# One written order for all engines in a test-time-trained linear layer and the feed-forward work laid between its rounds

## The chip, the cores and the metric

The kernel runs on one core of a Trainium2 chip. The time is the device time of one execution in microseconds (us); of several runs the median is given. PE is the matrix engine (TensorE), PEld its weight loads, DVE the vector engine, ACT the scalar engine, POOL GpSimd, SP the engine that issues most of the transfers.

## The reference

The program is a chain of eight blocks on `x` of shape (2, 1024, 256), each added to `x` after a normalization: two attention layers with a feed-forward each, a differential attention with a feed-forward, and at the end a linear model that is trained while it runs ("test-time training", TTT) with a last feed-forward. The change touches the TTT layer and the feed-forwards around it. Cut to what matters, for chunks of 16 tokens and 16 heads of width 16:

```python
def step(S, inp):                      # one chunk; 64 of them, one after the other
    qi, ki, vi, ei = inp
    kh = einsum('bchd,bhde->bche', ki, S)
    target = vi - ki
    mu = mean(kh, -1)
    rstd = rsqrt(var(kh, -1) + EPS)
    kh_hat = (kh - mu) * rstd
    g = w * kh_hat + b - target
    gw = g * w
    v_new = (gw - mean(gw, -1) - kh_hat * mean(gw * kh_hat, -1)) * rstd
    A = where(tri, einsum('bchd,bshd->bhcs', qi, ki), 0.0) * ei
    qh = einsum('bchd,bhde->bche', qi, S) - einsum('bhcs,bshe->bche', A, v_new)
    o = qi + _ln(qh, w, b)
    S = S - einsum('bchd,bche->bhde', ki * ei, v_new)
    return S, o
# before: q = silu(x Wq), k = x Wk scaled to unit length per head, v = x Wv,
#         beta = 2 sigmoid(x Wbeta)
# after:  o * sigmoid(x Wg1 Wg2), an RMS norm per head, then @ Wo
# feed-forward: (gelu(x Wg) * (x Wu)) @ Wd, 2048 hidden columns
```

The state `S` makes the 64 chunks a serial chain.

## The kernel before

Five stages follow each other; the last, `ttt_ffn1` (L1520), is the one in question. It has eight tiles of 2 x 128 tokens. Each tile has eight **rounds**, one per chunk of all heads, so there are 64 rounds. The pieces of work are closures that are called in some order:

- `ttt_inputs` (L1668) makes a tile's inputs: `begin` (normalization: statistics and root on DVE, scaling on POOL), `turn` (transposes, then ACT to `xT`), `keys` (projection to q and k, unit length of k), `targets` (values, then 16 small transfers `uk_d<-uk` through DRAM and one back into `r`, from which POOL makes `kp`), `diagonals` (transposes of k and q to `kqT`), `weights` (the products of keys and queries inside a chunk, `pa`, copied to `ag`), `low_ranks`, `rates`.
- `ttt_step` (L1859) is the heart of a round. `kh` is made of two products on PE, one from the state and one from the step `vs` before; ACT squares it, and some twenty small DVE operations follow (`rsqrt` alone has nine) to the new step `vs`.
- Around it a round has three more products of 16 small matmuls each (32x32 weights, 16 columns): the output's part from the state, `ds` for the state's update, and the output's part from `vs`. `ttt_product` (L1657) writes each of these; a product shows as 32 matmul instructions, and all as L1663.
- `ttt_outputs` (L1902) takes a finished tile through DRAM (17 transfers), normalizes it twice around the gate (`normalize`, nearly all on DVE), transposes and projects it, and adds it to `x`.
- `ffn1_tile` (L1959) is the feed-forward of a tile: `rows`, `turn`, eight `hidden` pieces (gate and up matmuls on PE, gelu on ACT, product on DVE) and four `down` pieces of eight matmuls.

In round n the products stand in the order output-from-state, `kh` from state, `kh` from `vs`, `ds`, output-from-`vs`; then come the pieces of `fill[n]` (L1615), written out by hand: outputs of the tile before, inputs of the tile after, and feed-forward of the tiles behind. The feed-forward of the previous layer's last tile is `owed`: its first three hidden pieces are laid between the inputs of tile 0, the rest in the rounds of the first two tiles.

Only PE runs in the written order here (L1590). DVE, ACT and POOL are ordered by the scheduler of the language, which takes what is ready by its own model and lays instructions of independent pieces between each other. The stages before use `in_order()` (L335), which holds PE, DVE, ACT and POOL in the written order. The SP queue is never held by hand.

The buffer for normalized tokens, `xT`, has two copies, and the PSUM buffer `gen`, through which most input and output pieces pass, has two.

Of the kernel before, what the change touches and what calls it, by code (L numbers as in the profile page):

```python
# [10 lines left out]
F32 = mybir.dt.float32  # L11
# [3 lines left out]
ALU = mybir.AluOpType  # L15
# [24 lines left out]
def interleave_into(out, a, b):  # L40
# [58 lines left out]
    "unpack": (-7.9, 2.57, (6.7, 7.6, 10.3, 13.8)),  # L99
}  # L100


class Net:
# [1416 lines left out]
    def ttt_ffn1(self, w, deq):  # L1520
# [11 lines left out]
        with ExitStack() as ctx:  # L1532
# [57 lines left out]
            ctx.enter_context(tc.manual_schedule(engines={mybir.EngineType.PE}))  # L1590
            data, inputs = self.ttt_inputs(0)
            owed = self.ffn1_tile(NB - 1, deq)
            begin, turn, keys, targets, diagonals, ag01, ag23, low_ranks, rates = inputs
            for piece in (
                begin, turn, keys, owed[0], targets, owed[1], diagonals, owed[2], ag01, owed[3],
                ag23, low_ranks, owed[4], rates,
            ):
                piece()
            vs = self.ttt_step(0, data, None)
            outputs = ffn = last_ffn = [lambda: None] * 20  # L1600
            nothing = [lambda: None]
            owed_by_tile = [
                nothing * 5 + [
                    owed[5], *nothing, owed[6], *nothing, owed[7], *nothing, owed[8], *nothing,
                    owed[9],
                ],
                nothing * 8 + [*nothing, owed[10], *nothing, *owed[11:14]],
            ]
            for i in range(NB):
                next_data, inputs = None, [lambda: None] * 9  # L1610
                if i < 2:
                    last_ffn = owed_by_tile[i]
                if i + 1 < NB:
                    next_data, inputs = self.ttt_inputs(i + 1)
                fill = [  # L1615
                    [outputs[0], inputs[0], *last_ffn[5:7], inputs[1]],
                    [last_ffn[7], inputs[2]],
                    [*last_ffn[8:10], inputs[3]],
                    [last_ffn[10], inputs[7], outputs[1]],
                    [last_ffn[11], outputs[2], ffn[0], inputs[4]],  # L1620
                    [last_ffn[12], inputs[8], inputs[5], inputs[6]],
                    [last_ffn[13], ffn[1], ffn[2]],
                    [ffn[3], ffn[4]],
                ]
                pq = ps.tile([P, 8, 4, D], F32, tag="pq", name="pq")
                for n in range(8):
                    S, vs_n = t.S, vs
                    self.ttt_product(
                        pq[:, n], lambda g: data.kq[:, 2 * n + 1, g, :], lambda g: S[:, g, :],
                        n == 0,  # L1630
                    )
                    if n < 7:
                        vs = self.ttt_step(n + 1, data, vs_n)
                    ds_ = ps.tile([P, 4, D], F32, tag="ds", name="ds")
                    self.ttt_product(
                        ds_, lambda g: data.kp[:, 4 * n + g, :], lambda g: vs_n[:, g, :],
                        True, True,
                    )
                    t.S = work.tile([P, 4, D], F32, tag="S", name="S", bufs=3)
                    nc.vector.tensor_tensor(t.S, S, ds_, ALU.add)  # L1640
                    self.ttt_product(
                        pq[:, n], lambda g: data.ag[:, n, g, 0, :], lambda g: vs_n[:, g, :], False
                    )
                    if n == 7:
                        qh = work.tile([P, 8, 4, D], F32, tag="qh", name="qh")
                        nc.scalar.copy(qh, pq)
                        if i + 1 < NB:
                            vs = self.ttt_step(0, next_data, None)
                    for piece in fill[n]:
                        piece()  # L1650
                outputs = self.ttt_outputs(i, data, qh)
                last_ffn, ffn = ffn, self.ffn1_tile(i, deq)
                data = next_data
            for piece in outputs[:1] + last_ffn[5:14] + outputs[1:] + ffn:
                piece()
# [12 lines left out]
    def ttt_inputs(self, i):  # L1668
# [5 lines left out]
        t_ = type("tile", (), {})()  # L1674
# [3 lines left out]

        def begin():
            t_.xn = self.layernorm_rows(work, (i, NB + i))  # L1680

        def turn():
            pt = gen("ln_t").rearrange("p (k t) -> p k t", k=2)
            t_.xT = self.layernorm_turn(work, pt, t_.xn, False)

        def to_diagonal(kind, src, scale):

            pt = gen("kq_t").rearrange("p (g n c) -> p n g c", g=4, c=D)
            for b in range(B):
                by_f = work.tile([P, 2, 8, D], F32, tag="by_f", name="by_f")  # L1690
                nc.scalar.activation(
                    by_f.rearrange("p f h d -> p h f d"), src(b), AF.Copy, scale=scale
                )
                for f in range(2):
                    nc.tensor.transpose(
                        pt[:, :, 2 * b + f, :], by_f[:, f].rearrange("p h d -> p (h d)"),
                        self.ident,
                    )
            for j in range(2):
                nc.scalar.activation(  # L1700
                    t_.kqT[:, :, kind, :, j, :], pt, AF.Copy, scale=t.half[:, j : j + 1]
                )

        def keys():
            q = t_.q = work.tile([P, B, C], F32, tag="q", name="q")
            k = work.tile([P, B, C], F32, tag="k", name="k", bufs=1)
            uk = t_.uk = work.tile([P, B, 8, 2, 2, D], F32, tag="uk", name="uk", bufs=1)
            for b in range(B):
                pqk = gen("pqk")
                self.project(pqk, t_.xT, b, w["wqkv"], 0, 512)  # L1710

                nc.scalar.activation(q[:, b], pqk[:, 0:C], AF.Tanh, scale=0.5)
                nc.vector.scalar_tensor_tensor(
                    q[:, b], q[:, b], 1.0, pqk[:, 0:C], ALU.add, ALU.mult
                )
                nc.scalar.copy(k[:, b], pqk[:, C : 2 * C])
            sq = work.tile([P, B, C], F32, tag="sq", name="sq", bufs=1)
            rk = work.tile([P, 32], F32, tag="rk", name="rk")
            nc.scalar.activation(sq, k, AF.Square)
            nc.vector.tensor_reduce(  # L1720
                rk, sq.rearrange("p b (h d) -> p (b h) d", d=D), AX.X, ALU.add
            )
            rk = self.rsqrt(work, rk, 1.0, 1e-6, "rk")
            nc.vector.tensor_scalar_mul(rk, rk, -1.0)
            kn = uk[:, :, :, :, 1, :].rearrange("p b h f d -> p (b h f) d")
            nc.vector.tensor_tensor(
                kn, k.rearrange("p b (h d) -> p (b h) d", d=D),
# [3 lines left out]
        def targets():  # L1731
            uk = t_.uk

            un = uk[:, :, :, :, 0, :].rearrange("p b h f d -> p b (h f) d")
            nc.vector.tensor_tensor(
                un, uk[:, :, :, :, 1, :].rearrange("p b h f d -> p b (h f) d"),
                w["ln_w"].rearrange("p (h d) -> p h d", d=D).unsqueeze(1)
                .to_broadcast([P, B, 16, D]), ALU.mult,
            )
            pv = gen("pv")  # L1740
            for b in range(B):
                out = pv[:, b * C : (b + 1) * C]
                nc.tensor.matmul(out, t.ones, t.wb, start=True, stop=False)
                for kc in range(2):
# [3 lines left out]
                    )  # L1748
            nc.vector.tensor_tensor(
                un, un, pv.rearrange("p (b n d) -> p b n d", b=B, d=D), ALU.add  # L1750
# [13 lines left out]
            )  # L1764
            kp = work.tile([P, 32, 2, D], F32, tag="kp", name="kp")
            for j in range(2):
                nc.gpsimd.tensor_scalar(
                    kp[:, :, j, :], r[:, :, 1, :], t.half[:, j : j + 1], 1.0, ALU.mult, ALU.mult
                )
            t_.kp = kp.rearrange("p m j d -> p m (j d)")  # L1770

        def diagonals():
            t_.kqT = work.tile([P, 8, 2, 4, 2, D], F32, tag="kqT", name="kqT")
            t_.kq = t_.kqT.rearrange("p n k g j c -> p (n k) g (j c)")
            to_diagonal(0, lambda b: t_.uk[:, b, :, :, 1, :], 1.0)
            to_diagonal(
                1, lambda b: t_.q[:, b, :].rearrange("p (h f d) -> p h f d", f=2, d=D), 0.5
            )
# [4 lines left out]
            t_.ag = work.tile([P, 8, 4, 2, 32], F32, tag="ag", name="ag")  # L1783

        def weights(pairs):

            ag, kq = t_.ag, t_.kq
            for pair in pairs:
                pa = gen("pa").rearrange("p (n g k c) -> p n g k c", n=2, g=4, k=2)
# [169 lines left out]
    def ffn1_tile(self, i, deq):  # L1959
# [7 lines left out]
        def rows():  # L1967
            f.xn = self.layernorm_rows(work, (i, NB + i))
# [190 lines left out]
```

## Time and profile before

| | us |
|---|---|
| median of 3 runs | 2913.81 (2906.41 to 2915.19) |
| profiled execution | 2906.75 |
| its span | 2905.0 |
| PE busy in the span | 2530.3 (87%) |
| DVE busy in the span | 2003.4 (69%) |
| `qh` copied at the end of tile 0 | 2198.7 |
| `qh` copied at the end of tile 7 | 2806.5 |

The stage under change begins at about 2090 us, when the stage before has added its last projection to `x` (DVE L1403 at 2089.31). The copy of `qh` marks the end of each tile's rounds; all eight lie at 2198.7, 2284.0, 2372.5, 2466.1, 2554.1, 2643.0, 2738.6 and 2806.5. After the last one stands the remaining feed-forward.

In the views that follow, a row of the table by stretches gives for each engine its busy time and, in brackets, its number of instructions; behind the engines stand the granted PE clock as a share of full speed, the share of busy DMA engines and the GB/s they moved. In the table of waits a row gives the waiting engine and line, what it waited for, the sum in us, how often, and the longest. "issue" is a wait for nothing that the profile shows. In a timeline a row gives start, duration, engine, line and operation.

### The profile page before, as it was taken

Reading aid. Unit: us, or ns where it says so; the run is one execution under the profiler, and the core shown is the slowest. Engines: PE = TensorE matmul, PEld = TensorE weight load, DVE = VectorE, ACT = ScalarE, POOL = GpSimd, SP = SyncE. Lnnn points to the kernel's source line nnn. Section 1 sums busy time; section 2 is a strip of 40 time slices with the busy share of each in tenths; the row PEclk is TensorE's granted clock in tenths of the full one; section 3 lists DMA queues with packets and bytes.
Section 4 is the critical chain, followed back from the end, with each engine's and each line's share of the span. In section 5 each row is a group of like instructions: output and inputs, shape, how many; then the busy total and the mean of one; then the engine's idle time right before and its main releaser. Section 6 shows DMA issues by size and latency. Waiting matters only on the chain.

```text
span 2905.0 us, 66838 instructions
## 1 busy us (share of the span) xinstructions
PE 2530.3 (87%) x26384; PEld 1572.5 (54%) x26384; DVE 2003.4 (69%) x6786; ACT 1329.8 (46%) x2800; POOL 1021.7 (35%) x1568
## 2 busy tenths in 40 slices
PE   6999998999998877988888888888787988898888
PEld 2334334444434444665555555555565776777777
DVE  5777774866758957778777878787657555665551
ACT  2676870345453335666666666757321211221110
POOL 3444242211106757667555655655300000000000
PEclk9999998999999967999999999999887998999999
DMA  3000000000001100000000000000011010110100
GB/s 121 1 1 1 1 1 0 1 1 1 1 1 53 36 1 1 1 1 1 1 1 1 1 1 1 1 1 1 20 31 25 10 25 21 21 31 18 24 9 15
DMA packets 61978, 35.37 MB, mean 12 GB/s; under 512 B 43216, under 2 KB 58080, under 8 KB 61664
## 3 DMA queue, kind: packets, MB, share of 16 engines
q1 hardware_dynamic: 59472, 29.49, 3.9%
q8 instruction: 207, 3.39, 0.5%
q10 hardware_dynamic: 2192, 1.61, 0.2%
q14 instruction: 107, 0.88, 0.1%
HBM read 22.68 MB, written 8.39 MB: 11 GB/s over the span
## 4 chain that ended last, share of the span: by engine, by line
PE 39%; DVE 13%; ACT 4%; POOL 4%; issue 4%; DMA 0%; POOLq 0%; ACTq 0%; DVEq 0%
PE ph L1484 5%; PE po L1993 5%; PE pg L1980 5%; PE pu L1980 4%; DVE p L1247 4%; PE e L1236 4%; PE dT L1308 3%; PE po L1503 2%; DVE p L1286 2%; PE py L1338 1%; POOL p L1294 1%; ACT p L1257 1%; POOL p L1274 1%; PE pq L1663 1%; PE kh L1663 1%
## 5 line engine op out<-in xcount | busy, mean ns | idle before, releaser
L1257 ACT ACTIVATE p<-p,nm 128x128 f32<-128x128 f32 (+7 forms) x512 | 390.8, 767 | 78.7 <-DVE nm L1253 40.9
L1247 DVE CUSTOM_DVE_ANT_0 p<-e,mask 128x512 f32<-128x512 f32 (+3 forms) x768 | 382.1, 551 | 59.5 <-PE e L1236 59.1
L1294 POOL TENSOR_SCALAR p<-p,md 128x128 f32<-128x128 f32 (+7 forms) x256 | 241.0, 945 | 175.5 <-DVE md L1286 147.4
L254 POOL TENSOR_SCALAR ln_mv<-ln_mv 128x2 f32<-128x2 f32 x64 | 15.7, 246 | 722.5 <-DVE ln_mv L252 709.6
L1322 ACT ACTIVATE pT<-dT 128x384 f32<-128x384 f32 (+3 forms) x384 | 176.2, 486 | 202.1 <-PE dT L1308 201.2
L1236 PE MATMUL e<-kT,qT 32*128 32x512 f32 (+3 forms) x1536 | 229.8, 578 | 44.3 <-DVE nm L1247 41.5
L1308 PE MATMUL dT<-ident,p 128*128 128x128 f32 x1152 | 197.0, 297 | 65.8 <-POOL p L1294 35.6
L1286 DVE CUSTOM_DVE_ANT_0 p<-p,nrs 128x128 f32<-128x128 f32 (+7 forms) x256 | 220.3, 885 | 24.7 <-POOL p L1278 24.4
L901 ACT ACTIVATE pr<-s 128x512 f32<-128x512 f32 (+3 forms) x384 | 157.3, 497 | 162.9 <-PE s L896 154.2
L1274 POOL TENSOR_SCALAR p<-p,ra,neg_lam 128x128 f32<-128x128 f32 (+7 forms) x256 | 217.8, 851 | 9.3
L1308 PEld LDWEIGHTS dT<-ident,p 128*128 128x128 f32 x1152 | 137.6, 149 | 153.1 <-POOL p L1294 67.7
L617 ACT ACTIVATE pr<-s 128x1024 f32<-128x1024 f32 (+1 forms) x192 | 145.3, 813 | 131.0 <-PE s L611 83.5
L1993 PE MATMUL po<-down,inter 128*128 128x256 f32 x576 | 160.1, 441 | 1.9 <-DVE x L2000 1.2
L861 PE MATMUL s<-kT,qT 32*128 32x512 f32 (+3 forms) x768 | 155.3, 519 | 3.8 <-DVE q_pad L869 1.9
L1980 PE MATMUL pg<-xT,gate 128*128 128x256 f32 x576 | 151.1, 409 | 5.5 <-ACT xT L283 5.5
L622 ACT ACTIVATE pr<-pr 128x1024 f32<-128x1024 f32 (+1 forms) x192 | 152.1, 852 | 0.0
L869 DVE CUSTOM_DVE_ANT_0 masked<-s,mask 128x128 f32<-128x128 f32 (+3 forms) x256 | 110.6, 487 | 58.9 <-PE s L861 58.8
L1236 PEld LDWEIGHTS e<-kT,qT 32*128 32x128 f32 x1536 | 84.8, 202 | 116.4 <-DVE nm L1247 74.3
L625 POOL TENSOR_SCALAR_AFFINE_SELECT pr<-pr 128x256 f32<-128x256 f32 x128 | 90.1, 722 | 154.7 <-ACT pr L622 57.7
L1986 DVE TENSOR_TENSOR inter<-inter,pu 128x512 f32<-128x512 f32 x72 | 49.3, 684 | 132.7 <-PE pu L1980 132.7
L1993 PEld LDWEIGHTS po<-down,inter 128*128 128x128 f32 x576 | 126.4, 224 | 25.0 <-DVE x L2000 2.0
L1980 PE MATMUL pu<-xT,up 128*128 128x256 f32 x576 | 139.3, 386 | 0.0
(295 smaller groups left out, 5377.2 us busy)
## 6 DMA issues: line engine op xcount, KB each, us to landing
uk_d<-uk SPq DMA_DIRECT2D x128, 32.0 KB, 1.9
r<-uk_d SPq DMA_DIRECT2D x8, 512.0 KB, 3.6
x<-in_L_attn_a_X SPq DMA_DIRECT2D x4, 512.0 KB, 6.9
qh_d<-qh SPq DMA_DIRECT2D x8, 256.0 KB, 2.6
o<-qh_d SPq DMA_DIRECT2D x128, 16.0 KB, 1.7
out<-x SPq DMA_DIRECT2D x4, 512.0 KB, 3.1
w<-in_L_ffn_W2T SPq DMA_DIRECT2D x1, 1024.0 KB, 7.5
pk<-in_L_ffn_gate_packed SPq DMA_DIRECT2D x8, 128.0 KB, 2.5
```

The source lines that it names most:

```text
L861: nc.tensor.matmul(tiles[g][:, 0:n], shared["qT"][rows, t, j * P : (j + 1) * P], kT[rows, lo : lo + n], start=True, stop=True,)
L901: nc.scalar.activation(pr[:, g, off:512], tiles[g][:, 0:m], AF.Exp, scale=0.25)
L1236: nc.tensor.matmul(own.tiles[h][:, a, 0 : hi - lo], made["q"][r : r + 32, a, t, :], kT[r : r + 32, a, lo:hi], start=True, stop=True,)
L1247: nc.vector.tensor_tensor_reduce(own.p[h][a][:, lo:hi], own.tiles[h][:, a, 0 : hi - lo], neg_row[:, T - nk + lo : T - nk + hi], -1.0, 3e38 ...
L1257: nc.scalar.activation(own.p[h][a], own.p[h][a], AF.Exp, bias=own.nm[:, h, a : a + 1], scale=-1.0, accum_out=own.sm[:, h, a : a + 1],)
L1274: nc.gpsimd.tensor_scalar(p1, p1, own.ra[:, h : h + 1], nlam[:, head : head + 1], ALU.mult, ALU.mult)
L1286: nc.vector.tensor_tensor_reduce(p0, p0, p1, own.nrs[:, h : h + 1], 3e38, ALU.add, ALU.min, own.md[:, h : h + 1],)
L1294: nc.gpsimd.tensor_scalar(p0, p0, -1.0, own.md[:, h : h + 1], ALU.mult, ALU.add)
L1308: nc.tensor.transpose(dT[:, n, :], own.p[h][0][:, kb * P : (kb + 1) * P], self.ident)
L1322: nc.scalar.activation(shared[t, s + h][:, lo:hi, :], own.dT[h, part][:, 0 : hi - lo, :], AF.Exp)
L1980: nc.tensor.matmul(ph[:, j, :], m_[:, kc, m * P : (m + 1) * P], f.xT[:, kc, :], start=(kc == 0), stop=(kc == 1),)
L1993: nc.tensor.matmul(f.po[:, b], inter[m // 2][:, m % 2, b * P : (b + 1) * P], wd[:, m % 2, (m // 2) * C : (m // 2 + 1) * C], start=(m == 0) ...
```

## The change

All four engines are held in the written order for the whole stage. For this the pieces are split where they change engine, so that a DVE part can stand later than the PE part that it reads: 32 pieces of inputs, 12 of outputs, 28 of feed-forward. A table gives each piece a time in rounds, relative to its tile; the ten parts of a round have fixed places 0.0 to 0.9 in it, and pieces are sorted among them.

- The round is now `K` (`kh` from state), `Q` (output from state), `k` (`kh` from `vs`), `q` (output from `vs`), `d` (`ds`), then the DVE parts `0` (ACT square, sum), `1` (root), `s` (state), `2` (gradient), `3` (finish to `vs`).
- The four `pa` products, before in one round, stand at 5.718, 7.26, 7.93 and 9.56 of the tile's time.
- `un = kn * ln_w` of the targets and the two operations `o * w_out`, `o + q` of the output gate go from DVE to POOL.
- `down` has eight pieces of four matmuls instead of four of eight; `xT` has four copies; `by_f` has one buffer per half.
- The feed-forward that is owed gets its own row; only its normalization and transposes stand ahead of round 0.

The diff, cut:

```diff
+TTT = {
+    "round": "K Q k q d 0 1 s 2 3",
+    "inputs": (
+        0.71, 1.04, 1.918, 1.923, 2.086, 2.518, 2.955, 2.923, 3.183, 3.82, 4.025, 2.963,
+        4.43, 5.74, 4.325, 4.74, 3.21, 5.132, 5.34, 5.718, 5.955, 7.26, 7.54, 7.93, 8.455,
+        9.56, 10.065, 3.663, 4.623, 5.719, 5.983, 6.765,
+    ),
+    "outputs": (0.58, 0.585, 1.55, 1.555, 1.66, 2.086, 2.6, 2.7, 2.958, 3.69, 4.43, 4.786),
+    "ffn": (
+        5.02, 5.025, 5.66, 6.618, 6.969, 7.618, 7.623, 9.118, 9.123, 9.618, 9.623, 10.618,
+        10.869, 11.55, 11.769, 12.518, 13.169, 13.618, 13.623, 7.774, 8.71, 9.95, 10.67,
+        11.974, 11.979, 13.674, 13.979, 14.084,
+    ),
...
+    "owed": (
+        -28.5, -25.1, -22.6, 1.263, 2.1, 2.43, 3.927, 3.932, 4.69, 5.645, 6.2, 7.709,
+        7.714, 8.663, 9.955, 10.527, 11.6, 11.865, 12.869, 3.932, 4.54, 6.946, 7.747, 9.96,
+        11.32, 13.23, 13.87, 14.91,
+    ),
+}
...
-            ctx.enter_context(tc.manual_schedule(engines={mybir.EngineType.PE}))
+            ctx.enter_context(self.in_order())
...
+                for m, step in zip(times, inputs):
+                    add(n + m if i else m - 30, step)
+                n += 16
+                outputs = self.ttt_outputs(i, data)
...
+            for n in range(8 * NB):
+                i, m = n // 8, n % 8
+                steps = self.ttt_round(i, m, tiles)
+                tokens = TTT["round"].split()
+                fill = sorted(at.pop(n, []), key=lambda x: x[0])
+                for k, token in enumerate(tokens):
+                    while fill and (fill[0][0] - n) * len(tokens) <= k + 1e-6:
+                        fill.pop(0)[1]()
+                    if token in steps:
+                        steps[token]()
+                for _, step in fill:
+                    step()
...
+        def by_w():
+
             for b in range(B):
+                nc.gpsimd.tensor_tensor(
+                    t_.uk[:, b, :, :, 0, :].rearrange("p h f d -> p (h f) d"),
+                    t_.uk[:, b, :, :, 1, :].rearrange("p h f d -> p (h f) d"),
+                    w["ln_w"].rearrange("p (h d) -> p h d", d=D), ALU.mult,
+                )
...
+        def gate():
+            o = data.o
+            nc.gpsimd.tensor_tensor(
+                o, o, t.w_out.unsqueeze(1).to_broadcast([P, B, C]), ALU.mult
+            )
+            nc.gpsimd.tensor_tensor(o, o, data.q, ALU.add)
...
+        return [stats, rows, turn] + [
+            lambda m=m, s=s: s(m) for m in range(8) for s in (hidden, gated)
+        ] + [lambda b=b, q=q: down(q, b) for q in range(4) for b in range(B)] + [add]
```

The order of the pieces in the three rows is that of the lists that the functions return. Inputs: `stats, begin, turn, keys0, silu0, keys1, silu1, squares, norms, normalize, by_w, values, targets, halves, by_half0, diagonals0, by_half1, diagonals1, bias`, then `products` and `weights` four times in turn, `low_rank` twice, `rates, own_rates, gates`. Outputs: `move, squares, norms, root, gate, open, squares, norms, root, turn, project, add`. Inputs of tile i+1 count from the first round of tile i; outputs and feed-forward of tile i from the first round of tile i+1. The row of the last two feed-forwards ("last") is left out above; they end behind round 63, the last one whole.

## The prediction

> **What bounds it now.** I read the stage from 2089.7 us by stretches cut at the copies of `qh` (tile 0, tile 1, the five tiles that are alike, the last, the tail), then PE's waits in the five tiles, then timelines of a bad round and of a clean one.
>
> ```profile
> 2089.70:2132.50 42.80, 32.97 (x356) 22.66 (x356) 18.64 (x79) 12.39 (x25) 6.47 (x14) 0.80 0.12 26
> 2132.50:2198.70 66.20, 56.33 (x1633) 44.67 (x1632) 41.39 (x199) 14.27 (x35) 1.54 (x2) 0.82 0.08 19
> 2198.70:2284.00 85.30, 66.36 (x1650) 49.12 (x1650) 53.72 (x248) 14.27 (x35) 3.87 (x8) 0.76 0.10 21
> 2284.00:2738.60 454.60, 401.48 (x8804) 321.93 (x8808) 273.49 (x1262) 91.80 (x211) 18.10 (x37) 0.93 0.10 22
> 2738.60:2806.50 67.90, 60.11 (x1457) 51.36 (x1458) 44.21 (x218) 9.42 (x21) 1.28 (x3) 0.97 0.05 11
> 2806.50:2905.00 98.50, 87.20 (x384) 73.99 (x384) 23.30 (x59) 11.87 (x20) 1.28 (x3) 0.95 0.06 17
> ```
>
> PE (first pair) is busiest everywhere, DVE (third) at 60%. A like tile takes 454.6/5 = 90.9 us. Stretches in which neither a matmul nor a weight load runs sum to 52.8 us, 10.5 a tile; the clock of 0.93 loses 6.4, some 5.8 of it while PE works. Left: 74.6 us of work. So at most some 16 us a tile can go. The waits say what the 10.5 are:
>
> ```profile
> PE pq L1663 <- issue: 12.8, 8, 2.2
> PE kh L1663 <- DVE vs L1899: 7.4, 5, 1.9
> PE kq_t L1695 <- ACT by_f L1691: 7.1, 10, 1.0
> PE ds L1663 <- issue: 6.9, 4, 2.5
> PE pa L1663 <- issue: 5.5, 5, 1.5
> PE kh L1663 <- issue: 4.7, 2, 2.6
> ```
>
> "issue" rows sum to 30.6 with a single 0.7, 6.1 a tile. All stand in small matmuls, worst where the four `pa` run on into a round:
>
> ```profile
> 2443.91 2.56 PE L1663 MATMUL pa<-kqT 32*32 32x64 f32 x146
> 2447.68 1.56 PE L1663 MATMUL pa<-kqT 32*32 32x64 f32 x108 [1.20 <-issue]
> ...
> 2451.15 0.29 PE L1663 MATMUL pq<-S,kqT 32*32 32x16 f32 x11 [1.74 <-issue]
> ```
>
> The wait for `vs` (1.5 a tile) comes from DVE. The scheduler lays big operations between the chain's:
>
> ```profile
> 2488.14 0.22 DVE L1885 TENSOR_TENSOR hat<-kh,rsq_y 128x64 f32<-128x64 f32 x1
> 2488.28 0.68 DVE L1937 TENSOR_TENSOR o<-o,q 128x512 f32<-128x512 f32 x1
> 2488.88 0.22 DVE L1889 TENSOR_TENSOR gp<-hat,w 128x64 f32<-128x64 f32 x1
> 2489.01 0.68 DVE L1938 SCALAR_TENSOR_TENSOR o<-sg,o 128x512 f32<-128x512 f32 x1
> ...
> 2493.17 0.22 DVE L1899 TENSOR_TENSOR vs<-gp,rate 128x64 f32<-128x64 f32 x1
> ```
>
> From `hat` to `vs` 5.25 us. Undisturbed, the whole chain:
>
> ```profile
> 2651.79 0.22 DVE L1882 TENSOR_REDUCE var<-k_sq 128x4 f32<-128x64 f32 x1 [0.44 <-ACT k_sq L1881]
> ...
> 2653.83 0.22 DVE L1885 TENSOR_TENSOR hat<-kh,rsq_y 128x64 f32<-128x64 f32 x1
> ...
> 2655.84 0.23 DVE L1899 TENSOR_TENSOR vs<-gp,rate 128x64 f32<-128x64 f32 x1
> ```
>
> 4.28 us, 2.24 of them from `hat`.
>
> **The like tile after the change.** No matmul is added or removed: what can change is when PE waits. I write each round as two sums and take the longer. PE, at full clock: product 0.27, hidden piece 3.45 (16 matmuls by 0.216), `down` 1.71, keys half 1.71, values 3.36, `pa` 1.0, low rank 0.9, transposes 0.45 to 0.6, projection 1.75, rates 1.05, gates 0.86. DVE: 0.8 from `k` to the sum (kh and ACT), chain 4.35, a root with scaling 2.45 (nine dependent operations 0.2 apart, and 0.65), 128x512 operations 0.62 to 0.65, normalization root 1.8, statistics 1.1.
>
> The eight rounds, PE / DVE: 6.5 / 6.3; 9.8 / 10.5; 11.6 / 7.1; 9.7 / 8.4; 8.4 / 6.0; 10.8 / 7.2; 5.7 / 5.4; 8.5 / 8.6. Two examples. Round 1: PE has `k q d` 0.8, `products(3)` 1.0, hidden 3.45, `turn` 0.55, `keys(0)` 1.71, `down` 1.71, then `K Q` 0.54: 9.8, to which the wait of `keys(0)` for ACT's `xT` adds 0.8. DVE starts 2.2 late (normalization root 1.8 and `gated` come first), then has 0.25, the output's `norms` 0.65 and `root` 2.45, 2.0, `gated` 0.62 and 2.3: 10.5. So 10.6. Round 7: `gated` stands ahead of `s`, `2` and `3`, and waits until PE has ended the hidden piece, 1.5 us, so DVE has 8.6. The longer ones sum to 71.9, PE's own list to 71.0; the trace has 74.6 of work for that list, so I scale to 75.5.
>
> To this I add what the written order cannot hide. `low_rank` stands right ahead of the outputs' `turn` while `values` still holds the other `gen` buffer until `targets`: 0.8. Clock: the nearest row is the attention stage, ordered so already and as full of PE work, at 0.96 and 0.97: 2.7. "issue" and POOL, next. ACT: `squares(0)` of the outputs stands behind its 17 transfers, and the next gelu and `kh` square behind it; `o` landed 13.6 us after the copy of `qh` started (2284.0 to 2297.6), which is some 15 after the start of round 7, where rounds 7 and 0 take 15.1: it costs nothing, but a later landing would cost its whole delay. SP is not held, and its order (17 transfers of `targets`, 17 of `move`) stays. No wait on `vs` or `by_f` is left in the sums, since PE work stands in front of it; where that cover fails, `vs` is next.
>
> **Issue.** The page's row "q8 instruction" (207 packets, 3.39 MB) makes 64 bytes for each of PE's 52768 instructions and 255 of them a packet, so PE's program comes in blocks. A round has 320 small ones in 1.3 us, four `pa` 512 more. [...] The rounds' own burst stays and `products(2)` still meets one, so I leave 3.5.
>
> **POOL.** DVE loses three operations (2.05 us a tile), POOL gains `by_w` and `gate`. The nearest POOL rows: 128x512 tensor_tensor 1.15 to 1.48, 128x256 0.72 to 1.03; so about 2.4 and 1.7. `gate` has from `root` to `open`, 4 us and more; `by_w` from `normalize` to `targets`, about 2: both hidden. [...]
>
> ```profile
> 2105.88 1.11 POOL L263 TENSOR_SCALAR ln_xn<-x,ln_mv,rsq_y 128x256 f32<-128x256 f32 x2 [6.83 <-DVE rsq_y L239]
> 2106.13 0.35 DVE L241 TENSOR_TENSOR rsq_w<-rsq_z,rsq_n 128x32 f32<-128x32 f32 x1
> ```
>
> 0.35 instead of 0.19. [...] Most gate time falls in round 1, the one that DVE bounds. I take 1.5.
>
> Sum: 75.5 + 0.8 + 3.5 + 1.5 + 2.7 = 84.0, a gain of 6.9 a tile, **34.5** for five.
>
> **The ends.** Opening: without the three hidden pieces (some 13 us there, partly at half clock) the first `K` comes at about 2119. But `r` landed at 2122.3 before, and `by_w` on POOL makes it 1.3 later; the gradient waits for it, and `vs` comes at about 2125.7. Round 0 then has no filler. The first eight rounds, by the same sums: 61.3, 66.5 with scale and clock, and the copy of `qh` 7.5 ahead of their end: with 2 for issue about 2187 against 2198.7, **12** gained, but 5 us more PE work is left over. Tile 1: 65 by the sums (that work in it), 72 with the additions, against 85.3 (18.8 of it PE gaps, clock 0.76): **13**. Last tile 65 against 67.9: **3**. Tail: same work; the last feed-forward's statistics now stand behind the `add` of the one before, while that addition's PE work is over, so the 3.7 us wait for normalized tokens grows: **-1.5**.
>
> 34.5 + 12 + 13 + 3 - 1.5 = 61. The profiled execution took 2906.75, the median is 7 above: 2846 for its like, **2850** (2852.8, rounded) for a median. Only POOL's operations add work, so nothing but waits can make it slower.
>
> **Rivals.** (a) Better: issue gaps all go, the clock stays at 0.97 and POOL hinders nobody. Then a tile takes 78.5: 62 + 12 + 13 + 5 = 92, 2822. For it: PE's own list is nearly gapless. Against: the bursts of the rounds stay. (b) Little: the gaps only change place, as issue gaps would if they hang on the number of blocks and not on bursts; a tile takes 88, 14.5 + 5 + 8: 2886. For it: of thirteen long issue gaps in the timeline five lie in plain rounds. (c) Slower: the strict DVE queue becomes the bound. Per tile 8 x 5.15 for the chain, 27.8 for the rest without overlap (now the scheduler runs two roots 0.11 apart instead of 0.2), 3.7 for POOL: 72.7. Fourteen DVE operations a tile wait for a product of PE or ACT (`gated`, `silu`, `weights`) and hold the whole chain behind them. At 1.3 us each the tile is back at 90.9; at 1.6 it is 95.1: 6 x 4.2 lost, 6 won at the start, 1.5 at the end: 2927 to 2934. For it: DVE now waits 2.7 us on average for `pu` (115.4 us in 42 waits), at no cost. Against: in the table most stand behind enough DVE work; I found one real wait of 1.5.
>
> **Numbers.** Forecast 0.55, (a) 0.17, (b) 0.14, (c) 0.11, no change 0.03. Within 0.3% (9 us) is about what a measurement of this kernel cannot tell from no change. Faster 0.86, same 0.03, slower 0.11. Range: from beyond (a), with POOL gain and no lock, 2805, to beyond (b), 2898; (c) and half of the rest are out.
>
> **What would show it.** Copies of `qh` 84 us apart; "issue" on PE near 3.5 a tile and none in four `pa` in a row; the chain `var` to `vs` never interrupted in its last 2.3 us; POOL operations of the gate at 1.2 with stretched DVE ones beside them; first `vs` at about 2126 behind `r`. I am wrong if PE's wait for `vs` grows beyond 2 us a tile, or if the DVE queue shows long waits for `pu` inside the chain.

## The result, and the profile after

| | us |
|---|---|
| before, median of 4 runs | 2910.11 (2904.48 to 2915.19) |
| after, median of 4 runs | 2864.29 (2861.26 to 2866.77) |
| ratio | 0.9849, 95% interval 0.9822 to 0.9875 |
| profiled execution after, its span | 2866.77, 2865.0 |

The change gains 46 us where the sum had 61; the time lies in the range, 14 above the forecast. One run of v4 below (3222.44 us, at a clock of 0.727) was slow and stands in no median here. The table by stretches of the changed kernel, cut at its own copies of `qh` (tile 0, tile 1, the five like tiles, the last, the tail; columns as in the prediction):

```profile
2094.20:2196.00 101.80, 79.86 (x1848) 56.78 (x1850) 56.53 (x254) 22.71 (x53) 8.39 (x15) 0.77 0.09 18
2196.00:2270.60 74.60, 66.51 (x1711) 50.28 (x1701) 56.89 (x249) 16.58 (x39) 8.23 (x12) 0.91 0.11 24
2270.60:2684.70 414.10, 389.69 (x8818) 306.96 (x8808) 296.93 (x1260) 91.37 (x210) 43.24 (x62) 0.97 0.11 26
2684.70:2760.30 75.60, 66.30 (x1573) 55.08 (x1564) 48.66 (x219) 10.29 (x24) 3.82 (x5) 0.91 0.04 10
2760.30:2865.00 104.70, 89.69 (x412) 75.24 (x400) 22.07 (x59) 11.89 (x20) 3.83 (x5) 0.91 0.05 16
```

The five tiles fell from 454.6 to 414.1. The last tile and the tail, behind them, **grew** from 67.9 and 98.5 to 75.6 and 104.7, with a clock of 0.91 where it had been 0.97 and 0.95. DVE is busier in the five tiles than before (296.93 against 273.49), though it lost operations to POOL: added up one by one, its operations take nearly the same (322 and 319 us, worked out from the traces), but the scheduler had laid more of them over one another. PE's waits in the five tiles:

```profile
PE ds L1726 <- issue: 8.5, 6, 1.8
PE pqk L327 <- ACT xT L320: 3.4, 5, 0.7
PE o_t L2069 <- ACT th L1910: 2.3, 5, 0.5
PE kh L1726 <- DVE vs L2013: 2.3, 9, 0.3
PE kh L1726 <- issue: 2.1, 1, 2.1
PE pq L1726 <- issue: 2.0, 1, 2.0
PE pa L1726 <- issue: 1.6, 1, 1.6
```

The "issue" rows (one more has 0.5) sum to 14.7, from 30.6; the wait for `vs` fell from 7.4 to 2.3, the one for `by_f` is gone.

But the chain on DVE did **not** get shorter. DVE between `hat` and `vs` in round 4 of a like tile, and POOL beside its end:

```profile
2396.43 0.23 DVE L1992 TENSOR_TENSOR hat<-kh,rsq_y 128x64 f32<-128x64 f32 x1
...
2398.32 0.69 DVE L2125 TENSOR_TENSOR inter<-inter,pu 128x512 f32<-128x512 f32 x1 [1.54 <-PE pu L2115]
2398.92 0.22 DVE L1999 TENSOR_TENSOR gp<-hat,w 128x64 f32<-128x64 f32 x1
...
2402.12 0.69 DVE L1810 TENSOR_TENSOR uk<-k,rsq_y 128x512 f32<-128x512 f32 x1
...
2403.73 0.65 DVE L2011 TENSOR_TENSOR gp<-gp,hat 128x64 f32<-128x64 f32 x1
```

```profile
2402.89 1.42 POOL L1818 TENSOR_TENSOR uk<-uk,ln_w 128x256 f32<-128x256 f32 x2 [25.11 <-DVE uk L1810]
```

A `gated` that waits 1.54 for PE, and a whole root with its scaling, stand inside the chain because the table put them there: 8 us instead of 2.24. One of these us is POOL's: `by_w` runs beside the end of the chain, and the operation shown last takes 0.65 and the one before it 0.77, where both take 0.22 otherwise. So it goes in each of the five tiles. From the start of `hat` to the end of `vs`, the mean over the 40 rounds of the five tiles is 2.87 us before and 4.37 after, worked out from the trace. In these tiles PE hardly waits for it (2.3 us), since the table also puts PE work in front of each `vs`.

The matmuls of the five tiles are the same in both kernels, so I split each stretch in three, from the trace: time in which neither a matmul nor a weight load runs ("idle"), clock lost (the sum of length times one minus the granted clock), and the rest, which is the work:

| us (idle, clock lost) | before | after | the change in a second run (c0_change) |
|---|---|---|---|
| opening, to `qh` of tile 0 | 109.0 | 101.8 | 103.1 |
| tile 1 | 85.3 | 74.6 | 74.4 |
| five tiles | 454.6 (52.8, 32.4) | 414.1 (24.3, 11.9) | 414.5 (23.6, 13.7) |
| last tile | 67.9 (7.8, 1.7) | 75.6 (9.3, 6.8) | 75.6 (9.5, 6.8) |
| tail | 98.5 (11.1, 5.1) | 104.7 (14.9, 9.1) | 104.5 (14.7, 9.1) |
| stage | 815.3 | 770.8 | 772.2 |

For the five tiles the split takes the clock lost while PE stood idle away twice (4 us before, hardly any after); without that the rest is 373 before and 378 after. Why the same matmuls took some 5 us more stays open.

The stage gained 44.5 and 43.1. The profiled executions differ by 40.0 (2906.75 to 2866.77): the stages before it, which the change doesn't touch, took 4.5 longer in that one.

### The profile page after: what moved, and what is told of

It is laid out like the page before. It is cut to its first block, busy times and chain, and to the rows that moved or that the text cites. A ratio compares the mean times of both kernels' runs of the same rounds, so it can differ in the third digit from the quotient of the medians.

```text
span 2865.0 us, 66910 instructions
## 1 busy us (share of the span) xinstructions
PE 2520.3 (88%) x26384; PEld 1555.7 (54%) x26384; DVE 2028.8 (71%) x6762; ACT 1330.0 (46%) x2800; POOL 1063.2 (37%) x1600
## 4 chain that ended last, share of the span: by engine, by line
PE 38%; DVE 14%; POOL 4%; ACT 4%; issue 3%; SPq 1%; DMA 1%; ACTq 0%; POOLq 0%; DVEq 0%
PE ph L1521 6%; PE pg L2115 5%; PE e L1273 4%; DVE p L1284 4%; PE pu L2115 4%; PE po L2133 3%; PE dT L1345 3%; PE po L1540 2%; DVE p L1323 2%; POOL p L1331 1%; PE py L1375 1%; POOL p L1311 1%; ACT p L1294 1%; PE kh L1726 1%; PE pq L327 1%
## 5 line engine op out<-in xcount | busy, mean ns | idle before, releaser
L1345 PE MATMUL dT<-ident,p 128*128 128x128 f32 x1152 | 197.1, 297 | 65.2 <-POOL p L1331 36.6
L1345 PEld LDWEIGHTS dT<-ident,p 128*128 128x128 f32 x1152 | 138.0, 149 | 153.5 <-POOL p L1331 67.9
L2115 PE MATMUL pg<-xT,gate 128*128 128x256 f32 x576 | 158.6, 423 | 4.6 <-ACT inter L2120 3.4
L2133 PE MATMUL po<-down,inter 128*128 128x256 f32 x576 | 144.2, 395 | 5.8 <-DVE inter L2125 5.8
L2120 ACT ACTIVATE inter<-pg 128x512 f32<-128x512 f32 x72 | 43.0, 597 | 195.7 <-PE pg L2115 195.7
L2115 PEld LDWEIGHTS pg<-xT,gate 128*128 128x128 f32 x576 | 116.5, 209 | 27.1 <-issue 4.7
L300 POOL TENSOR_SCALAR ln_xn<-x,ln_mv,rsq_y 128x256 f32<-128x256 f32 x128 | 89.8, 710 | 108.1 <-DVE rsq_y L279 88.8
```

The costliest lines, as they stand in the source:

```text
L1345: nc.tensor.transpose(dT[:, n, :], own.p[h][0][:, kb * P : (kb + 1) * P], self.ident)
L2115: nc.tensor.matmul(ph[:, j, :], m_[:, kc, m * P : (m + 1) * P], f.xT[:, kc, :], start=(kc == 0), stop=(kc == 1),)
L2133: nc.tensor.matmul(f.po[:, b], inter[m // 2][:, m % 2, b * P : (b + 1) * P], wd[:, m % 2, (m // 2) * C : (m // 2 + 1) * C], start=(b == m ...
```

## The experiments

All start from the changed kernel, except v10, which starts from the one before. "Against the change" is the median beside the `c0_change` run of the same group; where the group is another, it is the difference of the ratios times 2910.

**The change itself**, again, as the base of the others.

> The change itself, on the same chip as the three variants sent with it, as the ruler for them. 2864 us within 9, some 45 below the kernel before.

2865.37, ratio 0.9847 (0.983 to 0.9865): the result repeats.

**Only PE held**, as before the change, but with the new table.

```diff
-            ctx.enter_context(self.in_order())
+            ctx.enter_context(tc.manual_schedule(engines={mybir.EngineType.PE}))
```

> The new table, but only PE held in the written order; DVE, ACT and POOL ordered by the scheduler again. If the gain comes from the new order on PE (pieces spread, pa products apart), this stays within 10 us of the change, at most 2875. If it comes from the held DVE queue, which keeps big operations out of the chain from hat to vs, most of the 45 us are lost again: 2890 to 2910, with PE waiting for vs 5 us a tile or more.

2838.70, ratio 0.9752 (0.9732 to 0.9772): 27 us **faster** than the change. Its table by stretches (the profile is of the fastest of its four runs, 7 us below their median):

```profile
2094.10:2191.60 97.50, 77.59 (x1852) 55.73 (x1852) 57.78 (x273) 22.97 (x55) 9.36 (x18) 0.81 0.09 19
2191.60:2259.50 67.90, 62.69 (x1706) 48.03 (x1695) 51.53 (x250) 16.11 (x40) 9.36 (x14) 0.95 0.15 35
2259.50:2663.80 404.30, 381.33 (x8816) 300.08 (x8807) 264.07 (x1248) 91.41 (x210) 38.06 (x57) 0.99 0.11 25
2663.80:2734.10 70.30, 62.48 (x1580) 52.32 (x1568) 42.53 (x214) 10.32 (x24) 3.85 (x5) 0.98 0.05 11
2734.10:2829.60 95.50, 85.61 (x404) 73.14 (x392) 21.69 (x59) 11.73 (x20) 3.83 (x5) 0.97 0.06 17
```

Every stretch is shorter than with the change, and the clock is 0.95 to 0.99 from tile 1 on. In the five tiles idle time is the same (22.7 against 23.6) and the lost clock is not (3.4 against 13.7). The waits of PE there:

```profile
PE ds L1726 <- issue: 4.6, 4, 1.7
PE po L2133 <- DVE inter L2125: 4.3, 6, 0.9
PE pqk L327 <- ACT xT L320: 3.4, 5, 0.7
```

No row for `vs` is left at all, and from `hat` to `vs` the free scheduler needs 2.74 us in the mean. So holding DVE, ACT and POOL is no part of the gain; it gives 27 us back. The whole gain, and more, comes from what v1 keeps of the change: the new order on PE, and with it the split pieces, the four copies of `xT` and the `by_f` buffer per half. No run takes these apart, so how much of the 7.1 us of `by_f` waits went by the buffers alone is not shown.

**Which of the three engines.** Two kernels, each with one of them free:

```diff
-            ctx.enter_context(self.in_order())
+            ctx.enter_context(tc.manual_schedule(engines={mybir.EngineType.PE, mybir.EngineType.DVE, mybir.EngineType.Pool}))
```

> PE, DVE and POOL held in the table's order, ACT ordered by the scheduler. With PE alone held the kernel took 2839, with all four 2865. If ACT's queue behind the transfers is what costs the 27 us, this comes to 2840 to 2850; if DVE's written order does, it stays at 2860 or above.

2871.74, ratio 0.9859 (0.9836 to 0.9883): nothing gained. With `Activation` in the place of `DVE`, so that DVE is free:

> PE, ACT and POOL held, DVE ordered by the scheduler. If the held DVE queue costs the 27 us (small dependent operations 0.2 apart that nothing fills, and pieces that wait for PE), this comes to 2840 to 2850; if ACT's does, it stays at 2858 or above.

2853.53, ratio 0.9789 (0.9765 to 0.9812): 12 us (by medians) to 17 us (by ratios) faster than the change. Its last tile takes 68.2 and its tail 98.6, so holding DVE is what cost at the end; but its five tiles stay at 420.4 with 15.4 of clock lost. The remaining 10 to 15 us come only when ACT and POOL are free too, and ACT alone gives nothing. POOL alone was not freed. Why they go together stays open.

**POOL's operations back on DVE** (`by_w`, and both of `gate`).

```diff
-                nc.gpsimd.tensor_tensor(
+                nc.vector.tensor_tensor(
...
-            nc.gpsimd.tensor_tensor(o, o, data.q, ALU.add)
+            nc.vector.tensor_tensor(o, o, data.q, ALU.add)
```

> The three operations a tile that went to POOL (by_w, and two of the gate) go back to DVE, all else as in the change. By my sum POOL's share costs 1.5 us a tile through stretched DVE operations and saves 2.05 us of DVE, of which only the round that DVE bounds feels any: within 6 us of the change. If POOL shuts DVE out for the whole of its 4.1 us a tile, this is 12 to 20 us faster. If DVE's load bounds the rounds, it is 10 to 16 us slower.

2859.12, ratio 0.9823 (0.9805 to 0.984): 6 us faster than the change, though the two intervals overlap. What it takes away is seen in the changed kernel. POOL and, in the view of DVE, the root beside it:

```profile
2705.43 1.27 POOL L2056 TENSOR_TENSOR o<-o,w_out 128x512 f32<-128x512 f32 x1 [36.77 <-DVE rsq_n L269]
2706.78 1.27 POOL L2059 TENSOR_TENSOR o<-o,q 128x512 f32<-128x512 f32 x1
```

```profile
2705.41 0.17 DVE L270 TENSOR_SCALAR rsq_y<-rsq_n 128x4 int32<-128x4 int32 x1
2705.62 1.11 DVE L273 TENSOR_TENSOR rsq_z<-rsq_y 128x4 f32<-128x4 f32 x1
2706.76 0.16 DVE L274 TENSOR_TENSOR rsq_w<-rsq_z,rsq_n 128x4 f32<-128x4 f32 x1
2706.96 1.11 DVE L275 SCALAR_TENSOR_TENSOR rsq_z<-rsq_w 128x4 f32<-128x4 f32 x1
```

Two DVE operations end where the POOL operation ends, 1.11 us instead of 0.16. Over tiles 1 to 7 the stretched DVE operations lose 22.7 us, 2.5 in this variant. But the variant also gives DVE its three operations back, some 15 us in these tiles: DVE is busy there for 395.8 us instead of 402.5 (worked out from the traces, against c0_change). That is 7 us less in all, close to the 6 that the result shows.

With DVE free the same edit, on top of "only PE held":

> PE alone held, and the three POOL operations back on DVE: both of the variants that beat the change, together. If their gains add, 2839 - 6 = 2833; if the free scheduler has already hidden what POOL cost, within 3 us of 2839.

2834.24 (2828.43 to 2846.08), ratio 0.9755 (0.9732 to 0.9778), the same as without the edit. With DVE free, little of its work stands beside POOL's: in v1 the stretched operations of tiles 1 to 7 lose 5.7 us, against 22.7, and DVE waits 11.0 us in the five tiles for the `o` of `gate`, at no cost in time that this pair of runs shows.

**The four `pa` products together again**, in the new table, as in the kernel before.

```diff
-        4.43, 5.74, 4.325, 4.74, 3.21, 5.132, 5.34, 5.718, 5.955, 7.26, 7.54, 7.93, 8.455,
-        9.56, 10.065, 3.663, 4.623, 5.719, 5.983, 6.765,
+        4.43, 5.74, 4.325, 4.74, 3.21, 5.132, 5.34, 5.951, 5.952, 5.953, 5.954, 5.955, 5.956,
+        5.957, 5.958, 3.663, 4.623, 5.959, 5.983, 6.765,
```

> The four pa products of a tile stand in a row at the end of one round (5.951 to 5.958 with their weights, rates behind them), as before the change. If issue gaps come from bursts of small matmuls, they rise from about 2 us to 5 us a tile or more and the time by 15 to 25 us. If they only depend on how many instructions there are, the time stays within 6 us.

2890.99, ratio 0.9938 (0.992 to 0.9955): 26 us slower than the change. That looked as if spreading `pa` were most of the gain. But "issue" in the five tiles is 15.7, hardly above the 14.7 and 13.9 of the change; the edit also puts four pairs of `ag` operations into the held DVE queue at one place. So the same edit with only PE held:

> PE alone held, and the four pa products in a row at the end of one round. With four engines held this cost 25 us, but the issue gaps rose by only 2 us in five tiles. If it is the burst of small matmuls that costs, the issue waits rise here by 10 us or more in five tiles and the time by 15 to 25. If what cost was the pa weights standing in the held DVE queue ahead of the chain, then here the time rises by less than 8 us.

2847.05, ratio 0.9789 (0.9767 to 0.9811): 8 to 11 us on top of "only PE held" (by medians, by ratios), between the two outcomes expected, and the intervals overlap by a hair. "issue" is 14.3 against 13.8, the clock lost in the five tiles 10.2 against 3.4. And the other way round, the kernel before with `pa` spread over three rounds (cut; the rest of the edit makes four pieces of the two):

```diff
...
-                    [last_ffn[12], inputs[8], inputs[5], inputs[6]],
-                    [last_ffn[13], ffn[1], ffn[2]],
-                    [ffn[3], ffn[4]],
+                    [last_ffn[12], inputs[10], inputs[5]],
+                    [last_ffn[13], inputs[6], ffn[1], ffn[2]],
+                    [inputs[7], ffn[3], inputs[8], ffn[4]],
...
```

> The kernel before with one thing of the change: the four pa products apart, one in round 5, one in round 6, two with a hidden piece between them in round 7. If bursts make the issue gaps, their 37 us between the first and last copy of qh fall to 25 or less and the time falls by 10 to 20; if not, within 6 us of the kernel before.

2898.96, ratio 0.9973 (0.9955 to 0.9991): 8 us. "issue" in the five tiles falls from 30.6 to 22.1, but from the first copy of `qh` to the last it stays (37.2 and 36.8). Spreading `pa` is worth 8 to 11 us, from either end; the other 15 or so of v3 appear only while DVE, ACT and POOL are held.

**The old order inside the round**, with only PE held.

```diff
-    "round": "K Q k q d 0 1 s 2 3",
+    "round": "Q K k d q 0 1 s 2 3",
```

> PE alone held, all as in that variant (2839), but the five products of a round in the order of the kernel before: Q K k d q. If the round's new order is part of the gain, the issue waits of the five like tiles rise from 13.8 us toward 30 and the time by 8 us or more; if only the places of the pieces around the rounds count, within 5 us.

2838.11, ratio 0.9766 (0.9746 to 0.9787): no difference to v1 that is clear of the noise (0.6 less by medians, 4 more by ratios). The order of the products inside a round is not the cause.

**The end of the stage.** PE's waits in the tail of the changed kernel:

```profile
PE ln_t L315 <- POOL ln_xn L300: 4.5, 1, 4.5
PE pg L2115 <- ACT inter L2120: 3.4, 1, 3.4
PE pg L2115 <- ACT xT L320: 0.7, 1, 0.7
```

The first is the last feed-forward's normalization, which stands behind the last `add` of the one before. PE around it:

```profile
2803.76 3.44 PE L2133 MATMUL po<-down,inter 128*128 128x256 f32 x14
2811.66 1.24 PE L315 MATMUL ln_t<-ident,ln_xn 128*128 128x128 f32 x4 [4.46 <-POOL ln_xn L300]
2813.58 3.78 PE L2115 MATMUL pg<-xT,gate 128*128 128x256 f32 x8 [0.69 <-ACT xT L320]
2817.16 3.11 PE L2115 MATMUL pu<-xT,up 128*128 128x256 f32 x8
2820.10 1.89 PE L2115 MATMUL pg<-xT,gate 128*128 128x256 f32 x8
```

Behind the gap eight such matmuls take 3.78 and 3.11 instead of 1.89: 4.5 us of waiting cost 3.1 more, at a granted clock of 0.72 and 0.77 in the two stretches of 10 us from 2805. This stall is not new. The kernel before has it too, with a wait of 3.72:

```profile
2853.11 1.24 PE L278 MATMUL ln_t<-ident,ln_xn 128*128 128x128 f32 x4 [3.72 <-POOL ln_xn L263]
2855.04 3.78 PE L1980 MATMUL pg<-xT,gate 128*128 128x256 f32 x8 [0.69 <-ACT xT L283]
2858.61 3.01 PE L1980 MATMUL pu<-xT,up 128*128 128x256 f32 x8
```

To take it away, the statistics, the scaling and the transposes were put earlier, ahead of that `add` and of the `down` pieces that it ends:

```diff
-            20.04, 20.6, 20.85, 30.5, 32.9, 33.08, 33.9, 34.08, 34.085, 35.64, 35.745,
+            4.79, 4.795, 6.0, 30.5, 32.9, 33.08, 33.9, 34.08, 34.085, 35.64, 35.745,
```

> Statistics, root and transposes of the last feed-forward stand right behind the add that they need, instead of behind the add of the feed-forward before. The wait of 4.5 us for normalized tokens goes, and with it some half clock: 4 to 7 us faster than the change. If other work merely takes its place, within 2 us.

2860.68, ratio 0.9824 (0.9801 to 0.9847). In its tail, 95.3 instead of 104.5, PE waits once:

```profile
PE pg L2115 <- ACT inter L2120: 3.1, 1, 3.1
```

The wait is gone, and with it most of the lost clock (2.8 instead of 9.1). Of the 9 us the result shows 5 to 7 (by medians, by ratios), within overlapping intervals; the five tiles happened to take 3.3 more in its profile.

The second wait is ACT's. ACT in the tail of the changed kernel:

```profile
2762.51 0.60 ACT L2120 ACTIVATE inter<-pg 128x512 f32<-128x512 f32 x1 [1.58 <-PE pg L2115]
2773.54 0.63 ACT L2042 ACTIVATE o_sq<-o 128x512 f32<-128x512 f32 x1 [10.44 <-DMA o<-qh_d]
2774.08 0.58 ACT L2120 ACTIVATE inter<-pg 128x512 f32<-128x512 f32 x1
```

ACT stands still for 10.44 us at a square of the last outputs, whose data is on its way through DRAM; the gelu behind it was due, and PE's next `pg` waits 3.35 for its buffer, with slow matmuls behind the wait (the granted clock was 0.50 from 2775.25 to 2778.65):

```profile
2774.71 3.29 PE L2115 MATMUL pg<-xT,gate 128*128 128x256 f32 x8 [3.35 <-ACT inter L2120]
2777.79 2.32 PE L2115 MATMUL pu<-xT,up 128*128 128x256 f32 x8
```

This wait the kernel before did not have. For the last tile the square, and what follows it up to the second root, were put behind that gelu:

```diff
-                times = TTT["outputs"]
+                times = TTT["outputs"] if i < NB - 1 else (
+                    0.58, 1.835, 1.87, 1.875, 1.88, 2.824, 2.83, 2.88, 2.958, 3.69, 4.43, 4.786,
+                )
```

> In the last tile alone the output's squares, norms, root, gate and what follows stand later in the order, behind two more hidden pieces, so that ACT no longer waits 10 us for the 17 transfers with a gelu behind it. If that held queue caused the tail's 3.4 us stall of PE and the half clock after it, the tail (104.7 us in the change) falls by 4 to 8 and the time with it; if the tail is long for another reason, no change beyond 2 us.

2864.97, ratio 0.9842 (0.9817 to 0.9867): a miss. The tail fell by 2.9 to 101.6, where PE's 3.35 are gone but 2.2 for `o_t` have come, the last tile grew by 3.7 to 79.3, and nothing is left. That PE waits there for ACT is seen; that a better place would win the time back is not shown.

## Why the prediction was right, and where not

- **A like tile: right in size, with some luck in the parts.** 84.0 was the sum; 414.1/5 is 82.8: work 75.6 (75.5), idle 4.9 (5.8 for buffer, issue and POOL), clock 2.4 (2.7). But the 75.5 held 0.9 of waits beside PE's own 74.6, and that PE's work itself came to 75.6 is the unexplained growth above. And the clock, the largest single gain, was taken over from another stage and not worked out. "Issue" is 2.9 a tile where I left 3.5, `low_rank` before `turn` 0.46 where I had 0.8, `xT` 0.68 where I had 0.8. Forty us gained where 34.5 were forecast.
- **The reason for the issue gain: mostly wrong.** Spreading `pa`, on which it rested, is worth 8 to 11 us in the whole stage, and where only PE is held it leaves the issue gaps as they are (v9); v11 rules the round's own order out. The gaps fell by 3 us a tile through something else that v1 keeps of the change: which part of it is still open. The 3.5 that I left was an estimate, which no run shows; 2.9 was measured.
- **DVE held: the mechanism of rival (c), in part.** "The chain `var` to `vs` never interrupted" failed: from `hat` to `vs` takes 4.37 instead of 2.87. It did not become the bound that this rival made of it, since PE waits for `vs` only 2.3 us in five tiles. So of the two signs of being wrong, the waits for `pu` inside the chain came and the waits for `vs` did not. But "nothing but waits can make it slower" hid a price: holding DVE, ACT and POOL costs 27 us against the same table with PE held alone (v1), 12 to 17 of which freeing DVE alone wins back (v7). I costed the change only against the kernel before, not against its own half.
- **POOL: longer stretches than the row of before, at a lower price.** The 1.5 a tile was my estimate, and no run shows it. In that row a stretch was 0.16 (0.35 instead of 0.19). With the change, beside each of the 14 `gate` operations in the stretches of tiles 1 to 7, a DVE operation took 1.11 instead of 0.16 and ended 0.02 behind POOL's, 0.95 lost each. `by_w`, forecast as hidden, stretches the chain itself by 1.0 a tile. DVE lost about 3 a tile, of which some 2 only offset what it had handed over, and the time 6 us in all (v2), under 1 a tile.
- **Opening: 12 forecast, 7.2 measured (5.9 in the repeat).** The first `vs` came 36.6 us after the stage's start, where 36.0 was forecast (2125.7 from 2089.7), but that was luck: it did not stand behind `r`.

```profile
2125.74 1.36 POOL L1858 TENSOR_SCALAR kp<-r,half 128x512 f32<-128x512 f32 x2 [10.20 <-DMA r<-uk_d]
2126.41 0.22 DVE L1987 TENSOR_REDUCE var<-k_sq 128x4 f32<-128x64 f32 x1 [0.46 <-ACT k_sq L1986]
2129.33 0.23 DVE L2000 TENSOR_TENSOR gp<-gp,r 128x64 f32<-128x64 f32 x1
```

  `r` had landed when POOL started on it, 31.5 after the stage's start and not 33.9, and the gradient that reads it came 3.6 us later without a wait. The first `K` was late instead: it came after 31.0, behind the `pa` products, where 29.3 was forecast. The eight rounds from `vs` to `qh` took 65, not 61.3: that term was undersized. With PE alone held the stretch takes 97.5 (v1).
- **Tile 1: 13 forecast, 10.7 measured.** 74.6, where I had 72.
- **Last tile: "65 against 67.9, 3" failed.** It took 75.6: 7.7 lost instead of 3 won, of which 5.1 are clock (6.8 lost, 1.7 before) and 1.5 idle time. Issue gaps (5.3 for three) and a 3.0 wait of `po` for `inter` stand in it. v7 (68.2) and v1 (70.2) show that the held DVE queue makes it. In it DVE waits 8.8 us for `pu` at `gated` pieces, against 1.7 with DVE free (v7), though the kernel before has 12.5 of that; that these waits hold the round's chain, now that DVE may not pass them, with little PE work left to cover it is my reading.
- **Tail: "-1.5" was mis-sized, -6.2 measured, and for other reasons.** The step forecast, statistics behind the last `add`, made the wait for normalized tokens 0.7 longer (4.46 from 3.72); the half clock behind it was there before (0.50 from 2850.6 to 2860.9 before, from 2809.4 to 2819.6 after). What v5 wins, 9 us of tail, is thus mostly an old stall. New are two things. "`squares(0)` ... costs nothing" was argued for the like tiles alone: in the tail no two rounds stand in front of the square, ACT waits 10.44 us, and PE 3.35 and then 1.8 more in slow matmuls. And "same work" did not hold at the very end: the new `add` does both halves of a tile behind the last matmul, where before the first half had left 8 us earlier, so 6.5 us stand behind PE's last matmul instead of 4.5. With the 0.7 these come to 7.9; 2.4 of small waits that the kernel before had in its tail are gone, which leaves 5.5 of the 6.2.

The five terms give 44.5 against 61: like tiles 6 better, opening 4.8, tile 1 2.3, last tile 10.7 and tail 4.7 worse. The forecast's direction and the size of its main term were right, and the miss is the ends, where I took the price of the steady state.

The fastest kernel in this study is the new table with PE alone held, 2838.70 and, with the three operations back on DVE, 2834.24: 2.5% below the kernel before.

## What to carry to other kernels

Hold in a written order the engine whose gaps cost, and leave the engines with many short dependent operations to the scheduler until a run with each freed has shown which order pays: here the new order on PE, with the buffers and split pieces that came with it, was worth 71 us, and holding the three others took back 27. A written order that fits the steady state must be followed separately through the first and the last tile, where an instruction that waits for a transfer or for another engine has no work in front of it and all that stands behind it on its engine waits too (here ACT for 10.44 us in the tail, with a gelu behind the square). A gap on PE is to be priced with the clock that follows it: here 4.5 us of waiting cost 7.6, at a granted clock of 0.72 and 0.77 in the two stretches of 10 us from 2805. And a stall in the tail is to be looked for in the kernel before, too, ahead of blaming the change for it.

## What the runs showed of the hardware

- **DVE beside POOL.** In the changed kernel a DVE operation with two SBUF inputs (`rsq_z<-rsq_y` or `rsq_z<-rsq_w`) took 1.11 or 1.12 us instead of 0.16 beside a 128x512 POOL multiplication or addition of 1.27 us, fourteen times in seven tiles. The operations that began 0.02 or 0.03 us ahead of POOL's took 0.17 (`rsq_y<-rsq_n`, one input) and 0.16 (`rsq_w<-rsq_z,rsq_n`, two). `rsq_n<-var`, with one input, took 0.46 instead of 0.17 beside `kp` (2126.66, to 0.03 past the end of the POOL operations shown above).
- **Granted clock and gaps.** In the five tiles the clock was 0.93 before, 0.97 with the change and 0.99 with PE alone held. From the change (c0_change) to v1 idle time in them stays within 1 us (23.6 and 22.7) while 10 us of lost clock go (13.7 to 3.4), so the sum of the gaps alone does not account for it. In the traces of before and after the records of granted clock in the stage read 1.0 or 0.5, and those of 0.5 begin whole multiples of 3.41 us apart. I cut the stage into pieces of that length, on the same starts. Where PE idled for more than 1.7 us within a piece at full clock, the next piece was at half clock in 23 cases of 23; where it idled for less than 0.5 us, in 2 of 287; in between in 15 of 72, and what decides there is open. The five tiles have nine gaps of 0.8 us or more with the change and ten in v1, and 7 pieces at half clock against 2.
- **Issue gaps and the instruction queue.** In the traces of before and after, each of the 35 issue gaps of 0.8 us or more between the first and the last copy of `qh` ends 1.2 to 1.6 us after a 16 KB packet of the instruction queue (q8) has landed, behind 208 to 360 PE instructions in the 2 us before it. PE's other waits of that length there end 0.34 or 1.78 to 8.66 us after one. No run isolates this; it is a coincidence in time.
- **Untouched stages move.** The stage began between 2088.1 and 2096.9 us in the profiles, though the code before it was the same, so terms of one profile below some 4 us say little without the others.
